# A graph and attention layer: where its rows are normalised and its edge lists made, and how its first chunks are multiplied

## The chip, the cores and the metric

The kernel runs on one core of a Trainium2 chip. The time is device microseconds (us) of one execution of the whole program. Engines are called as in the profile: PE (TensorE, matrix products), DVE (VectorE), ACT (ScalarE), POOL (GpSimd), SP (SyncE, which here only issues DMAs). The three timed runs of the kernel before took 3303.76, 3309.79 and 3318.09 us.

## What is computed

x has 10000 rows of 512 numbers (float32). There are 160000 edges, sorted by their destination.

```python
xn = layernorm(x)
# part 1: message passing
agg = segment_sum((xn @ W)[src] * edge_weight[:, None], dst)
# part 2: linear attention, 8 heads of 64
q, k, v = split(xn @ w_qkv.T)
q = softmax(q, within a head) * 64 ** -0.5
k = softmax(k, over all rows)
out = layernorm_gamma((k.T @ v per head, applied to q) @ w_out.T)
x = x + relu(agg + bias) + out
# part 3: six experts, mixed by a router that sees the mean of layernorm(x)
x = x + experts(layernorm(x))
```

The kernel sums messages of xn itself and multiplies by W afterwards, and it forms the exponentials of q and k without subtracting a maximum. For that it needs a proof that these are small: the squared norm of each column of the weights of q and k is compared with a bound (7.0), and the answer, `usable`, is the scale of every exponential. If it is not fulfilled, or if the lists of edges are not as the fast path assumes, a branch in the middle (`general_path`) computes the general case; for these inputs it is not taken.

## The kernel before

Rows are cut into 20 chunks of 512 (128 partitions x 4 rows, the quarters; the last has 272), edges into 1250 tiles of 128.

**Rows.** `normal_rows(n)` brings in the next n chunks: SP loads x (L409), DVE forms mean and variance of each quarter (L157, L158) and adds epsilon (L160), POOL raises to the power -1/2 (L162), DVE forms the negative mean (L413), and then the quarters are normalised in place, two by POOL (L416) and two by ACT in two passes each (L419, L420). ACT's queue writes the chunk to `xn_d` in the chip's main memory (L421). The first KEPT = 2 chunks stay in buffers of their own; the others share the pool `a_io` of 4 buffers, and are read again later (`rows_of`, L800).

**First sweep over chunks.** Each chunk is transposed (`turned_rows`, L192), multiplied by the weights of k and q, and the exponentials are taken (ACT, L848). The first EARLY = 3 chunks do this with plain products (`times`, L200: 16 for k and 16 for q); the rest with Strassen's scheme in Winograd's form (`seven`, L234: 28 products), which needs sums of the weights (`kq_sum`, L224 to L227) and of the rows (`xs_b`, L217 to L220) on DVE. q is normalised on DVE (`softmax_rows`, L183 to L185), transposed, and stored in `qT_d`. `pc` (L871) adds k-transposed times xn to the context G.

**Norms of the weights.** Between K and Q of chunk 0, `norms` squares a weight on ACT, sums it over its rows on PE with a column of ones as the stationary operand (L591), and takes the largest on DVE; `as_they_are` compares, and spreads the answer over the partitions with one more product (L600).

**Edges.** `place_edges` loads four lists (source, weight, destination, first destination of each tile) and turns them on DVE into `place` (where within a window an edge adds), `bases` and `jump` (which window is where), and counts of what holds. `find_rows` finds for each chunk where its sums lie; `oddities` adds up the counts into `n_odd`, which `general_path` reads. Then come the tiles: for each, POOL gathers 128 rows of `xn_d` (L556, `msg`, 24 buffers), DVE writes a selection matrix (L562, L564), PE multiplies (L574, `pm`), ACT copies and stores the sums in `part_d` (L577, L578). Windows that reach over a boundary are joined by carries (L641, POOL's queue).

**Second sweep.** Attention's output (`po`, L200), the gathered sums of edges `at` (L963, an indirect DMA on POOL), their product with W (`pg`, L200), and x1 is stored. **Third stage:** the experts, on PE alone for nearly all of its time.

**What sets the order.** PE's instructions stand in the order in which they are written (`manual_schedule`). The orders of the other engines are set by a scheduler when the kernel is built; `behind(a, b)` tells it to put a behind b on one engine, without a wait. Each engine then runs its list strictly in order. `work(us)` is called after products, and paces two things by an estimate of PE's time: until `place_edges` has run it calls `normal_rows` so that rows are spread over the first chunks (by `EARLY_TOTAL`, with 2 chunks of lead), and from then on `edges_to`, which writes tiles into PE's order (PACE = 0.9 us per tile, from an offset of -6 tiles; PRODUCT = 0.83 us per product). Tiles not placed by the end of the first sweep go on in the second.

Of the kernel before, what the change touches and what calls it, by code (L numbers as in the profile page):

```python
# [9 lines left out]
F32 = mybir.dt.float32  # L10
# [18 lines left out]
EARLY = 3  # L29
ROWS_SOON = 5  # L30
# [20 lines left out]
def gps_layer_kernel(  # L51
# [59 lines left out]

    until = const.tile([P, P], F32, name="until")
# [40 lines left out]
    def row_stats(t, r, mv, on_pool=False):  # L153

        st = small.tile([P, SUB, nc.vector.BN_STATS_DIM], F32, name="st")
        for s in range(SUB):
            nc.vector.bn_stats(st[:r, s, :], t[:r, s, :])  # L157
# [12 lines left out]
        nc.vector.scalar_tensor_tensor(near[:r], near[:r], -0.5, ve[:r], op0=ALU.mult, op1=ALU.mult)  # L170
        nc.vector.scalar_tensor_tensor(mv[:r, :, 1], near[:r], 1.5, root[:r], op0=ALU.add, op1=ALU.mult)
# [210 lines left out]
    with ExitStack() as ph:  # L382
# [7 lines left out]
        ew = edge_ctx.enter_context(tc.tile_pool(name="edge_w", bufs=3))  # L390
# [11 lines left out]
        normal = []  # L402

        def normal_rows(n):
# [33 lines left out]
        n_big = ep.tile([1, 2], F32, name="n_big")  # L438
# [3 lines left out]
        def place_edges():  # L442
# [15 lines left out]
            nc.vector.tensor_copy(place, dst_sb)  # L458
# [54 lines left out]
        def find_rows(c, other):  # L513

            at = ew.tile([P, 1], F32, name="at")
            lo, hi = span(c)
            past = ew.tile([P, WIDEST], F32, name="past_c", bufs=1)[:, : hi - lo - 1]
# [28 lines left out]
        def edges_in(i):  # L546
# [12 lines left out]
            sel = ew.tile([P, 2 * GROUP, WIN], F32, name="sel", bufs=6)  # L559
# [8 lines left out]
        def edges_summed(i, batch, m, sel):  # L568
# [7 lines left out]
            part = ew.tile([P, D], F32, name="part")  # L576
# [8 lines left out]
        def norms(i, w):  # L585

            sq = b_io.tile([P, KB, D], F32, name="sq", tag="qT")
            nc.scalar.activation(sq, w, AF.Square)
            pn = psum_e.tile([1, D], F32, name="pn", tag="pm")
            for kb in range(KB):  # L590
                nc.tensor.matmul(pn, ones, sq[:, kb, :], start=kb == 0, stop=kb == KB - 1)  # L591
            nc.vector.tensor_reduce(n_big[:, i : i + 1], pn, axis=AX.X, op=ALU.max)

        def as_they_are():


            nc.vector.tensor_scalar(n_big, n_big, NORM2, None, op0=ALU.is_le)
            nc.vector.tensor_tensor(n_big[:, 0:1], n_big[:, 0:1], n_big[:, 1:2], ALU.mult)
            pn = psum_e.tile([P, 1], F32, name="pn", tag="pm")
            nc.tensor.matmul(pn, until[0:1, :], n_big[:, 0:1], start=True, stop=True)  # L600
            nc.vector.tensor_copy(usable, pn)

        def oddities():

            n_good = ew.tile([P, 1], F32, name="n_good", bufs=1)
# [3 lines left out]
            n = ew.tile([1, 2], F32, name="n", bufs=1)  # L609
            nc.vector.tensor_scalar(n[:, 0:1], pn, -1.0, float(ALL_GOOD), op0=ALU.mult, op1=ALU.add)  # L610
            nc.vector.tensor_scalar(n[:, 1:2], n_big[:, 0:1], -1.0, 1.0, op0=ALU.mult, op1=ALU.add)
# [10 lines left out]
        def carry_loads(i):  # L622
            on = ew.tile([P, PER, D], F32, name="on", bufs=1)
            nc.scalar.dma_start(on[:CHAINED], by_window[:CHAINED, i * PER : (i + 1) * PER, :])
            own = ew.tile([P, PER, D], F32, name="own", bufs=1)
# [3 lines left out]
        def carry_chained(i):  # L629
            on, own = held.pop("loads")  # L630
            same = ew.tile([P, P], F32, name="same", bufs=1)
# [20 lines left out]
        EARLY_TOTAL = PRODUCT * KB * EARLY * 3 * KB  # L652
# [160 lines left out]

        xn = rows_of(0)
        xnT = turned_rows(0, xn)
        for c, (_, r) in enumerate(chunks):
            if c == EARLY:
                normal_rows(NCH)
                place_edges()
                next_nodes()  # L820
                oddities()
                for soon in range(ROWS_SOON):
                    find_rows(soon, None)
                norm_ctx.close()
                done[1] = -6 * PACE
# [6 lines left out]
            if c < EARLY:  # L832
                for o, w in ((ek, wk), (qt, wq)):
                    sums = []
                    for s in range(SUB):
# [32 lines left out]
            for cb in range(KB):  # L868
# [4 lines left out]
                if c:  # L873
                    added = nc.vector.tensor_tensor(G[:, cb, :], G[:, cb, :], pc, ALU.add)  # L874
                else:
                    nc.vector.tensor_copy(G[:, cb, :], pc)
                work(SUB * PRODUCT)
                if cb == KB // 2 - 1:
                    qT = b_io.tile([P, KB, SUB * P], F32, name="qT")
                    transposed(qT, qt, r, psum, "ps")  # L880
                    nc.scalar.dma_start(qT_d[c], qT[:, :, : SUB * r])
            if c >= ROWS_SOON:
                find_rows(c, added)
            if c == EARLY - 2:
                for inst in sums_for([kq_sum[:, i] for i in range(4)], wk[:, :KH], wq[:, :KH], wk[:, KH:], wq[:, KH:]):
                    behind(inst, added)
# [524 lines left out]
```

## Time and profile before

| what | us |
|---|---|
| median of three runs | 3309.79 |
| profiled execution, its own time | 3313.32 |
| its span in the trace | 3311.6 |
| PE busy in the span | 3206.1 |
| POOL busy | 1387.6, of which gathers 1230.9 |
| DVE busy, ACT busy | 1773.9, 822.0 |
| first products of chunk 0 (K) | at 18.7 |
| products of chunk 3, the first with Strassen | at 178.8 |
| first gather; first tile's products | at 173.8; 194.5 |
| last gather | at 1857.5 |

The profile is one execution, recorded by the hardware. Its first part gives the busy time of each engine. The groups have one line for a source line, engine, operation and tile: "out<-in", the count, then busy us and mean ns of one, then the engine's idle time just before such instructions and what ended it. The view of waits gives, for one engine, what its instructions waited for: us in total, how often, the longest. A timeline gives start, length, engine, line, and in brackets the idle time before it with its releaser. A view of windows gives for each stretch the busy time of each engine (with the number of instructions), the granted clock of PE, the busy share of the 16 DMA engines and GB/s; where it is limited to a tile, the busy times are those of that tile's instructions.

### The profile page before, as it was taken

What the parts mean: (1) busy time and instruction counts of PE and PEld (TensorE: products, weight loads), DVE (VectorE), ACT (ScalarE), POOL (GpSimd) and SP (SyncE); (2) the same over time, 40 slices, a digit from 0 to 9 for tenths busy, and PEclk for the clock granted to TensorE, in tenths of its full rate; (3) what the DMA queues carried; (4) which work ended last, traced back from release to release, by engine and by line L of the source; (5) the groups of instructions that cost most, each with busy time, mean ns of one, the idle gap of its engine ahead of it and who ended that gap; (6) DMA issues with size and microseconds to landing.
All of it is one profiled execution on the core that took longest, in us unless ns stands there. A gap on an engine that the chain in (4) does not pass through costs nothing.

```text
span 3311.6 us, 36107 instructions
## 1 busy us (share of the span) xinstructions
PE 3206.1 (97%) x12779; PEld 1893.4 (57%) x12779; DVE 1773.9 (54%) x3935; ACT 822.0 (25%) x1664; POOL 1387.6 (42%) x1416
## 2 busy tenths in 40 slices
PE   6999999999999789999999989999999999999998
PEld 3444444444443233333333358888888888888886
DVE  7855556555553256565655666445544455445533
ACT  4422222222221112222222132222222222222211
POOL 6667777777777777777777400000000000000000
PEclk9999999999999999999999989999999999999999
DMA  8778888888878899999999822222121212122111
GB/s 320 286 254 267 273 281 290 283 260 278 277 243 278 295 318 353 340 351 345 341 339 340 246 96 60 56 67 74 51 64 51 89 51 64 51 78 63 52 39 40
DMA packets 216011, 654.39 MB, mean 198 GB/s; under 512 B 34405, under 2 KB 74341, under 8 KB 188107
## 3 DMA queue, kind: packets, MB, share of 16 engines
q0 software_dynamic: 105552, 360.05, 33.7%
q1 hardware_dynamic: 67800, 169.56, 15.5%
q10 hardware_dynamic: 42464, 122.32, 9.5%
q8 instruction: 105, 1.72, 0.2%
q14 instruction: 90, 0.74, 0.1%
HBM read 491.21 MB, written 166.63 MB: 199 GB/s over the span
## 4 chain that ended last, share of the span: by engine, by line
PE 88%; DMA 8%; DVE 2%; issue 1%; POOL 1%; ACT 0%; POOLq 0%; DVEq 0%; SPq 0%; ACTq 0%
PE px L234 15%; PE p L234 12%; PE pz L234 11%; PE py L234 10%; PE pm L574 9%; PE po L200 8%; PE pg L200 8%; PE pc L871 7%; DMA msg<-xn_d,src_sb 4%; PE pt L192 3%; PE ph L234 2%; PE pk L200 2%; DMA xn<-in_x 1%; DMA z_d<-xt 1%; DMA at<-part_d,row_of 1%
## 5 line engine op out<-in xcount | busy, mean ns | idle before, releaser
L556 POOL DMA_INDIRECT msg<-xn_d,src_sb x1250 | 1230.9, 985 | 425.2 <-issue 196.5
L574 PE MATMUL pm<-msg,sel 128*32 128x512 f32 x2504 | 372.6, 603 | 19.4 <-DMA msg<-xn_d,src_sb 17.6
L200 PE MATMUL po<-G,qT 128*128 128x512 f32 (+1 forms) x640 | 297.2, 610 | 18.3 <-DMA qT<-qT_d 18.3
L200 PE MATMUL pg<-wq,aT 128*128 128x512 f32 (+1 forms) x640 | 294.1, 606 | 0.0
L871 PE MATMUL pc<-xn,ek 128*128 128x512 f32 (+1 forms) x640 | 286.4, 596 | 0.7 <-DVE G L874 0.6
L577 ACT COPY part<-pm 128x512 f32<-128x512 f32 x217 | 126.9, 585 | 611.5 <-PE pm L574 603.4
L574 PEld LDWEIGHTS pm<-msg,sel 128*32 128x32 f32 x2504 | 69.1, 109 | 288.1 <-issue 186.3
L200 PEld LDWEIGHTS po<-G,qT 128*128 128x128 f32 (+1 forms) x640 | 116.3, 190 | 186.2 <-issue 162.6
L200 PEld LDWEIGHTS pg<-wq,aT 128*128 128x128 f32 (+1 forms) x640 | 115.5, 188 | 177.1 <-issue 162.2
L234 PE MATMUL px<-xnT,w_sb 128*128 128x256 f32 (+1 forms) x800 | 203.7, 377 | 11.3 <-DVE u L1228 11.1
L157 DVE BATCH_NORM_STATS2 st<-ot 128x6 f32<-128x512 f32 (+1 forms) x160 | 110.2, 689 | 190.8 <-ACT ot L1001 190.2
L871 PEld LDWEIGHTS pc<-xn,ek 128*128 128x128 f32 (+1 forms) x640 | 117.0, 190 | 142.1 <-issue 130.8
L234 PE MATMUL p<-kq_sum,xs_b 128*128 128x512 f32 (+1 forms) x408 | 189.5, 600 | 0.0
L234 PE MATMUL px<-w_sb,hh 128*128 128x256 f32 (+1 forms) x800 | 185.7, 379 | 0.0
L234 PE MATMUL py<-xs,w_sum 128*128 128x256 f32 (+1 forms) x800 | 185.0, 374 | 0.0
L234 PE MATMUL py<-w_sum,hh 128*128 128x256 f32 (+1 forms) x800 | 179.2, 379 | 0.0
L234 PEld LDWEIGHTS px<-xnT,w_sb 128*128 128x128 f32 x800 | 150.4, 191 | 32.7 <-DVE u L1228 13.1
L234 PEld LDWEIGHTS px<-w_sb,hh 128*128 128x128 f32 (+1 forms) x800 | 150.0, 188 | 22.7
L234 PEld LDWEIGHTS py<-w_sum,hh 128*128 128x128 f32 (+1 forms) x800 | 150.0, 188 | 22.7
L234 PEld LDWEIGHTS py<-xs,w_sum 128*128 128x128 f32 x800 | 149.4, 190 | 19.6
L345 ACT ACTIVATE xn<-xn,st_all 128x128 f32<-128x128 f32 x288 | 114.8, 481 | 99.8 <-DMA xn<-x_d 92.1
L234 PEld LDWEIGHTS p<-kq_sum,xs_b 128*128 128x128 f32 (+1 forms) x408 | 73.6, 187 | 109.7 <-issue 84.4
(299 smaller groups left out, 4649.8 us busy)
## 6 DMA issues: line engine op xcount, KB each, us to landing
part_d<-part ACTq DMA_DIRECT2D x217, 256.0 KB
msg<-xn_d,src_sb POOLq DMA_INDIRECT x1250
xn<-in_x SPq DMA_DIRECT2D x19, 1024.0 KB
xn_d<-xn ACTq DMA_DIRECT2D x19, 1024.0 KB
qT_d<-qT ACTq DMA_DIRECT2D x19, 1024.0 KB
qT<-qT_d SPq DMA_DIRECT2D x19, 1024.0 KB
xt<-in_x SPq DMA_DIRECT2D x19, 1024.0 KB
x_d<-ot SPq DMA_DIRECT2D x19, 1024.0 KB
```

The source lines that it names most:

```text
L157: nc.vector.bn_stats(st[:r, s, :], t[:r, s, :])
L192: nc.tensor.transpose(pt[:, s * r : (s + 1) * r], t[:r, s, kb * P : (kb + 1) * P], ident[:r, :r])
L200: nc.tensor.matmul(po[:r, :], t[:, kb, s * r : (s + 1) * r], w[:, kb, :], start=kb == 0, stop=kb == KB - 1)
L234: nc.tensor.matmul(o, lhs[j], rhs[j], start=start and j == 0, stop=stop and j == n - 1, skip_group_check=True)
L345: nc.scalar.activation(xn[:, s, b * P : (b + 1) * P], xn[:, s, b * P : (b + 1) * P], AF.Identity, bias=st[:, b, s, 0:1], scale=st[:, b, s, ...
L556: nc.gpsimd.indirect_dma_start(out=m[k], out_offset=None, in_=xn_d, in_offset=bass.IndirectOffsetOnAxis(ap=src_sb[:, t0 + k : t0 + k + 1], ...
L574: nc.tensor.matmul(pm[h * WIN : (h + 1) * WIN, :], sel[:, k, :], m[k] if k < len(m) else m[0], start=j == 0, stop=j == batch - 1, skip_gro ...
L577: nc.scalar.copy(part, pm)
L871: nc.tensor.matmul(pc, ek[:r, s, cb * P : (cb + 1) * P], xn[:r, s, :], start=s == 0, stop=s == SUB - 1)
```

## The change

- EARLY is 2: chunk 2, the third, uses Strassen's scheme. `kq_sum` is formed at the end of chunk 1 behind its first addition to G.
- The rows are normalised by ACT alone, one pass for each quarter with scale and bias; POOL forms the bias (minus mean times the power), and adds epsilon. DVE keeps only the statistics.
- `a_io` has 7 buffers (4 before); `normal_rows` runs with 4 chunks of lead (2 before), paced so as to be done after two chunks. Two more chunks are asked for before the first transposes.
- The loads of the lists are issued on SP before the load of chunk 4 (`edges_listed`); the work on DVE is put behind the last statistics of rows (chunk 19).
- `next_nodes` and `oddities` move to chunk 5, `find_rows` of chunks 0 to 4 to chunks 5 to 9. The pool for edge work opens later, after the rows' pool is closed; tiles start from an offset of -16.
- The squares of the weights are taken early, in two buffers. The norms are formed by columns: the squares are the stationary operand, ones the moving one, 16 products of one column for each weight; the comparison is made per column, summed, and added up over the partitions by a product with a matrix of ones.
- Chunks 0 and 1: all copies after transposes go to ACT.

In the kernel after, the same lines have other numbers (K and Q products at L204, Strassen at L238, transposes at L196, `pm` at L573, `qt`'s exponentials at L856).

```diff
-EARLY = 3
-ROWS_SOON = 5
+EARLY = 2
+ROWS_IN = 2
+CHECKED = 5
...
-            nc.vector.bn_aggr(mv[:r, s, :], st[:r, s, :])
+            last_stats = nc.vector.bn_aggr(mv[:r, s, :], st[:r, s, :])
         ve = small.tile([P, SUB], F32, name="ve")
-        nc.vector.tensor_scalar_add(ve[:r], mv[:r, :, 1], EPS)
+        (nc.gpsimd if on_pool else nc.vector).tensor_scalar_add(ve[:r], mv[:r, :, 1], EPS)
         if on_pool:
             nc.gpsimd.tensor_tensor(mv[:r, :, 1], ve[:r], half_neg[:r], ALU.pow)
-            return
+            return last_stats
...
-        ew = edge_ctx.enter_context(tc.tile_pool(name="edge_w", bufs=3))
+        a_io = norm_ctx.enter_context(tc.tile_pool(name="a_io", bufs=7))
         tmp = norm_ctx.enter_context(tc.tile_pool(name="edge_t", bufs=1))
-        a_io = norm_ctx.enter_context(tc.tile_pool(name="a_io", bufs=4))
...
-                row_stats(xt, r, mv, on_pool=True)
-                minus = small.tile([P, SUB], F32, name="minus")
-                nc.vector.tensor_scalar(minus[:r], mv[:r, :, 0], -1.0, None, op0=ALU.mult)
+                last_stats[0] = row_stats(xt, r, mv, on_pool=True)
+                nc.gpsimd.tensor_tensor(mv[:r, :, 0], mv[:r, :, 0], mv[:r, :, 1], ALU.mult)
+                nc.gpsimd.tensor_scalar(mv[:r, :, 0], mv[:r, :, 0], -1.0, None, op0=ALU.mult)
                 for i in range(SUB):
-                    if i % 2:
-                        nc.gpsimd.tensor_scalar(xt[:r, i, :], xt[:r, i, :], mv[:r, i, 0:1], mv[:r, i, 1:2],
-                                                op0=ALU.subtract, op1=ALU.mult)
-                    else:
-                        nc.scalar.activation(xt[:r, i, :], xt[:r, i, :], AF.Identity, bias=minus[:r, i : i + 1])
-                        nc.scalar.activation(xt[:r, i, :], xt[:r, i, :], AF.Copy, scale=mv[:r, i, 1:2])
+                    nc.scalar.activation(xt[:r, i, :], xt[:r, i, :], AF.Identity,
+                                         bias=mv[:r, i, 0:1], scale=mv[:r, i, 1:2])
...
-        wk = kvp.tile([P, KB, D], F32, name="wk")
-        nc.sync.dma_start(wk, w_qkv_t[:, D : 2 * D].rearrange("(k p) d -> p k d", p=P))
-        nc.sync.dma_start(wq, w_qkv_t[:, :D].rearrange("(k p) d -> p k d", p=P))
-        kq_sum = kvp.tile([P, 4, KH, D], F32, name="kq_sum", tag="wv_wo")
...
-        def place_edges():
+        def edges_listed():
             nc.sync.dma_start(src_sb, src)
             nc.sync.dma_start(w_sb, edge_w)
             dst_sb = tmp.tile([P, NET], I32, name="dst_sb", tag="whole")
             nc.sync.dma_start(dst_sb, dst)
             row_sb = tmp.tile([P, NET], I32, name="row_sb", tag="row")
             nc.sync.dma_start(row_sb, dst[0:1, :].to_broadcast([P, NET]))
-
-            nc.vector.tensor_scalar(row_sb, row_sb, 2, None, op0=ALU.arith_shift_right)
+            return dst_sb, row_sb
+
+        def place_edges(dst_sb, row_sb):
+
+            behind(nc.vector.tensor_scalar(row_sb, row_sb, 2, None, op0=ALU.arith_shift_right), last_stats[0])
...
-            nc.vector.tensor_copy(place, dst_sb)
+            behind(nc.vector.tensor_copy(place, dst_sb), last_stats[0])
...
-        def norms(i, w):
-
-            sq = b_io.tile([P, KB, D], F32, name="sq", tag="qT")
+        def squares_of(w, tag):
+            sq = b_io.tile([P, KB, D], F32, name="sq", tag=tag)
             nc.scalar.activation(sq, w, AF.Square)
-            pn = psum_e.tile([1, D], F32, name="pn", tag="pm")
-            for kb in range(KB):
-                nc.tensor.matmul(pn, ones, sq[:, kb, :], start=kb == 0, stop=kb == KB - 1)
-            nc.vector.tensor_reduce(n_big[:, i : i + 1], pn, axis=AX.X, op=ALU.max)
+            return sq
+
+        def norms(i, sq):
+
+            pn = psum_e.tile([P, KB], F32, name="pn", tag="pm")
+            for cb in range(KB):
+                for kb in range(KB):
+                    nc.tensor.matmul(pn[:, cb : cb + 1], sq[:, kb, cb * P : (cb + 1) * P], ones,
+                                     start=kb == 0, stop=kb == KB - 1)
+            nc.vector.tensor_scalar(small_norms[:, i], pn, NORM2, None, op0=ALU.is_le)
 
         def as_they_are():
 
 
-            nc.vector.tensor_scalar(n_big, n_big, NORM2, None, op0=ALU.is_le)
-            nc.vector.tensor_tensor(n_big[:, 0:1], n_big[:, 0:1], n_big[:, 1:2], ALU.mult)
+            n_small = small.tile([P, 1], F32, name="n_small", bufs=1)
+            nc.vector.tensor_reduce(n_small, small_norms, axis=AX.XY, op=ALU.add)
             pn = psum_e.tile([P, 1], F32, name="pn", tag="pm")
-            nc.tensor.matmul(pn, until[0:1, :], n_big[:, 0:1], start=True, stop=True)
-            nc.vector.tensor_copy(usable, pn)
+            nc.tensor.matmul(pn, all_ones, n_small, start=True, stop=True)
+            nc.vector.tensor_scalar(usable, pn, 2.0 * D, None, op0=ALU.is_ge)
...
-        EARLY_TOTAL = PRODUCT * KB * EARLY * 3 * KB
+        EARLY_TOTAL = PRODUCT * KB * ROWS_IN * 3 * KB
...
-                normal_rows(int(done[1] / EARLY_TOTAL * (NCH + 1)) + 2 - len(normal))
+                normal_rows(int(done[1] / EARLY_TOTAL * (NCH + 1)) + 4 - len(normal))
...
-            transposed(xnT, xn, chunks[c][1], psum, "ps")
+            transposed(xnT, xn, chunks[c][1], psum, "ps", by_act=range(KB) if c < EARLY else (1, 3))
...
+        wk = kvp.tile([P, KB, D], F32, name="wk")
+        nc.sync.dma_start(wk, w_qkv_t[:, D : 2 * D].rearrange("(k p) d -> p k d", p=P))
+        nc.sync.dma_start(wq, w_qkv_t[:, :D].rearrange("(k p) d -> p k d", p=P))
+        squared = [squares_of(wk, "qT"), squares_of(wq, "xs_b")]
+        kq_sum = kvp.tile([P, 4, KH, D], F32, name="kq_sum", tag="wv_wo")
+        normal_rows(2)
+        lists = edges_listed()
         xn = rows_of(0)
         xnT = turned_rows(0, xn)
         for c, (_, r) in enumerate(chunks):
             if c == EARLY:
                 normal_rows(NCH)
-                place_edges()
-                next_nodes()
-                oddities()
-                for soon in range(ROWS_SOON):
-                    find_rows(soon, None)
+                place_edges(*lists)
                 norm_ctx.close()
-                done[1] = -6 * PACE
+                pools["w"] = edge_ctx.enter_context(tc.tile_pool(name="edge_w", bufs=3))
+                done[1] = -16 * PACE
...
-                            norms(0, wk)
-                            norms(1, wq)
+                            norms(0, squared[0])
+                            norms(1, squared[1])
...
+                    if cb == 0:
+                        first_added = added
                 else:
                     nc.vector.tensor_copy(G[:, cb, :], pc)
                 work(SUB * PRODUCT)
                 if cb == KB // 2 - 1:
                     qT = b_io.tile([P, KB, SUB * P], F32, name="qT")
-                    transposed(qT, qt, r, psum, "ps")
+                    transposed(qT, qt, r, psum, "ps", by_act=range(KB) if c < EARLY else (1, 3))
                     nc.scalar.dma_start(qT_d[c], qT[:, :, : SUB * r])
-            if c >= ROWS_SOON:
+            if c == CHECKED:
+                next_nodes()
+                oddities()
+            if c >= CHECKED:
                 find_rows(c, added)
-            if c == EARLY - 2:
+                if c < 2 * CHECKED:
+                    find_rows(c - CHECKED, added)
+            if c == EARLY - 1:
                 for inst in sums_for([kq_sum[:, i] for i in range(4)], wk[:, :KH], wq[:, :KH], wk[:, KH:], wq[:, KH:]):
-                    behind(inst, added)
+                    behind(inst, first_added)
```

More of the change, by code (lines that the diff above doesn't have):

```diff
@@ L110, in gps_layer_kernel @@
                    allow_small_or_imprecise_dtypes=True)
+    all_ones = const.tile([P, P], F32, name="all_ones")
+    nc.gpsimd.memset(all_ones, 1.0)
     until = const.tile([P, P], F32, name="until")
@@ L397, in gps_layer_kernel @@
         norm_ctx = ph.enter_context(ExitStack())
+        a_io = norm_ctx.enter_context(tc.tile_pool(name="a_io", bufs=7))
         tmp = norm_ctx.enter_context(tc.tile_pool(name="edge_t", bufs=1))
-        a_io = norm_ctx.enter_context(tc.tile_pool(name="a_io", bufs=4))
         normal = []
+        last_stats = [None]
         def normal_rows(n):
@@ L437, in gps_layer_kernel @@
         count = ep.tile([P, 3 + len(AT_HAND) + 2 * NCH], F32, name="count")
-        n_big = ep.tile([1, 2], F32, name="n_big")
+        small_norms = ep.tile([P, 2, KB], F32, name="small_norms")
         usable = ep.tile([P, 1], F32, name="usable")
         n_odd = ep.tile([1, 1], I32, name="n_odd")
-        def place_edges():
+        def edges_listed():
             nc.sync.dma_start(src_sb, src)
@@ L513, in find_rows @@
         def find_rows(c, other):
-            at = ew.tile([P, 1], F32, name="at")
+            at = pools["w"].tile([P, 1], F32, name="at")
             lo, hi = span(c)
-            past = ew.tile([P, WIDEST], F32, name="past_c", bufs=1)[:, : hi - lo - 1]
+            past = pools["w"].tile([P, WIDEST], F32, name="past_c", bufs=1)[:, : hi - lo - 1]
             scan = nc.vector.scalar_tensor_tensor(
@@ L558, in edges_in @@
                             in_offset=bass.IndirectOffsetOnAxis(ap=src_sb[:, t0 + k : t0 + k + 1], axis=0))
-            sel = ew.tile([P, 2 * GROUP, WIN], F32, name="sel", bufs=6)
+            sel = pools["w"].tile([P, 2 * GROUP, WIN], F32, name="sel", bufs=6)
             if n < GROUP * batch:
@@ L575, in edges_summed @@
                                      start=j == 0, stop=j == batch - 1, skip_group_check=True)
-            part = ew.tile([P, D], F32, name="part")
+            part = pools["w"].tile([P, D], F32, name="part")
             nc.scalar.copy(part, pm)
@@ L583, in gps_layer_kernel @@
         held = {"edges": []}
-        def norms(i, w):
-            sq = b_io.tile([P, KB, D], F32, name="sq", tag="qT")
+        def squares_of(w, tag):
+            sq = b_io.tile([P, KB, D], F32, name="sq", tag=tag)
             nc.scalar.activation(sq, w, AF.Square)
-            pn = psum_e.tile([1, D], F32, name="pn", tag="pm")
-            for kb in range(KB):
-                nc.tensor.matmul(pn, ones, sq[:, kb, :], start=kb == 0, stop=kb == KB - 1)
-            nc.vector.tensor_reduce(n_big[:, i : i + 1], pn, axis=AX.X, op=ALU.max)
+            return sq
[6 more added lines that the diff above has]
+            nc.vector.tensor_scalar(small_norms[:, i], pn, NORM2, None, op0=ALU.is_le)
         def as_they_are():
-            nc.vector.tensor_scalar(n_big, n_big, NORM2, None, op0=ALU.is_le)
-            nc.vector.tensor_tensor(n_big[:, 0:1], n_big[:, 0:1], n_big[:, 1:2], ALU.mult)
+            n_small = small.tile([P, 1], F32, name="n_small", bufs=1)
+            nc.vector.tensor_reduce(n_small, small_norms, axis=AX.XY, op=ALU.add)
             pn = psum_e.tile([P, 1], F32, name="pn", tag="pm")
-            nc.tensor.matmul(pn, until[0:1, :], n_big[:, 0:1], start=True, stop=True)
-            nc.vector.tensor_copy(usable, pn)
+            nc.tensor.matmul(pn, all_ones, n_small, start=True, stop=True)
+            nc.vector.tensor_scalar(usable, pn, 2.0 * D, None, op0=ALU.is_ge)
         def oddities():
-            n_good = ew.tile([P, 1], F32, name="n_good", bufs=1)
+            n_good = pools["w"].tile([P, 1], F32, name="n_good", bufs=1)
             nc.vector.tensor_reduce(n_good, count, axis=AX.X, op=ALU.add)
@@ L608, in oddities @@
             nc.tensor.matmul(pn, n_good, ones, start=True, stop=True)
-            n = ew.tile([1, 2], F32, name="n", bufs=1)
+            n = pools["w"].tile([1, 2], F32, name="n", bufs=1)
             nc.vector.tensor_scalar(n[:, 0:1], pn, -1.0, float(ALL_GOOD), op0=ALU.mult, op1=ALU.add)
-            nc.vector.tensor_scalar(n[:, 1:2], n_big[:, 0:1], -1.0, 1.0, op0=ALU.mult, op1=ALU.add)
+            nc.vector.tensor_scalar(n[:, 1:2], usable[0:1], -1.0, 1.0, op0=ALU.mult, op1=ALU.add)
             nc.vector.tensor_tensor(n_odd, n[:, 0:1], n[:, 1:2], ALU.add)
@@ L622, in carry_loads @@
         def carry_loads(i):
-            on = ew.tile([P, PER, D], F32, name="on", bufs=1)
+            on = pools["w"].tile([P, PER, D], F32, name="on", bufs=1)
             nc.scalar.dma_start(on[:CHAINED], by_window[:CHAINED, i * PER : (i + 1) * PER, :])
-            own = ew.tile([P, PER, D], F32, name="own", bufs=1)
+            own = pools["w"].tile([P, PER, D], F32, name="own", bufs=1)
             nc.scalar.dma_start(own[:CHAINED], by_window[1 : CHAINED + 1, SUB + i * PER : SUB + (i + 1) * PER, :])
@@ L630, in carry_chained @@
             on, own = held.pop("loads")
-            same = ew.tile([P, P], F32, name="same", bufs=1)
+            same = pools["w"].tile([P, P], F32, name="same", bufs=1)
             nc.vector.scalar_tensor_tensor(same[:CHAINED, :CHAINED], bases[:CHAINED, 1 : CHAINED + 1], nexts[:CHAINED],
```

## The prediction

> **What bounds the kernel now.** I read the page first, then the waits of TensorE (PE), then its timeline.
>
> ```profile
> span 3311.6 us, 36107 instructions
> ...
> PE 3206.1 (97%) x12779; PEld 1893.4 (57%) x12779; DVE 1773.9 (54%) x3935; ACT 822.0 (25%) x1664; POOL 1387.6 (42%) x1416
> ...
> L556 POOL DMA_INDIRECT msg<-xn_d,src_sb x1250 | 1230.9, 985 | 425.2 <-issue 196.5
> ```
>
> PE is idle for 105 us of 3311.6. The 97% hides a second bound: the 1250 gathers on POOL, one per tile of edges. Their busy time in six stretches of 100 us of the first sweep:
>
> ```profile
> 174.00:274.00 100.00, 15.39 (x128) 3.34 (x128) 76.24 (x79) 1.00 0.83 264
> 274.00:374.00 100.00, 19.23 (x160) 4.17 (x160) 76.23 (x79) 1.00 0.85 271
> ```
>
> 79 gathers per 100 us, a pitch of 1.27 us, in every stretch: POOL never stops, and PE takes the tiles about as fast. The waits of PE say who is ahead:
>
> ```profile
> PE pm L574 <- DMA msg<-xn_d,src_sb: 17.6, 22, 1.8
> ...
> PE pn L600 <- DVE n_big L598: 9.2, 1, 9.2
> PE pt L192 <- DMA at<-part_d,row_of: 6.0, 1, 6.0
> ```
>
> The 22 waits for gathers begin at 961 us. From there to the last tile (1870 us) the chain of gathers sets the time; before and after it, PE's own work does. So two things count: when the gathers can start to flow, and how much PE work is left behind the last tile. Timelines of POOL (gathers) and PE (early part):
>
> ```profile
> 173.84 1.26 POOL L556 DMA_INDIRECT msg<-xn_d,src_sb  x1 [8.83 <-DMA xn_d<-xn]
> ```
> ```profile
> 51.93 0.58 PE L600 MATMUL pn<-n_big,until 1*128 1x1 f32 x2 [9.15 <-DVE n_big L598]
> 52.44 2.08 PE L200 MATMUL pk<-wq,xnT 128*128 128x512 f32 x2
> ...
> 86.45 13.90 PE L200 MATMUL pk<-wk,xnT 128*128 128x512 f32 x32
> ...
> 133.78 6.60 PE L200 MATMUL pk<-wk,xnT 128*128 128x512 f32 x15
> ```
>
> Chunk 0 ends at 86.45, chunk 1 at 133.78. Chunk 2 (plain) ends at 178.6.
>
> **The change, step by step.** T0 is the time at which PE begins the products of chunk 2, which are now Strassen's: 133.8 before.
>
> *Step 1, the first rows.* All four quarters of a chunk now go through ScalarE (ACT) once: 4 x 0.62 = 2.5 us, as much as two quarters twice before. POOL loses 2 x 2.07 us per chunk and gains three small operations that the trace doesn't show in this form; a 128x4 memset takes 0.10, the 128x4 power 1.03, so between 0.3 and 3.1 per chunk. They resemble the 0.10 row (plain arithmetic): 0.3. DVE loses two of 0.07 pitch. These edits are hidden by the loads. But in the built order ACT has the rows of chunks 0 to 3 and both squares (1.9 each) ahead of the four copies that turn chunk 0. The x of chunk 3 lands at 23.3 (its first statistics); + 2.8 statistics + 1.5 POOL + 2.5 ACT = 30.1, + 0.6 copy: K of chunk 0 starts at 30.8, against 18.68. With its 15.0 us it ends at 45.8.
>
> *Step 2, norms.* 64 records with one column. The nearest row is the sum of the keys at the end of the sweep (8 records in 0.95 us): 64 x 0.119 = 7.6 us, against 2 x 3.59 = 7.2; the squares are ready long before. They end at 53.4. Then PE waits for the count on DVE, and behind that wait stand all products of Q. On DVE the count stands, in the built order, behind three quarters of the statistics of chunk 10. What must have moved by then: eleven chunks of x (11.5 MB), two weights (2.1), four lists (2.6), constants (0.7), 16.9 MB read, with 4.2 to 7.3 MB written. The rate at this place is 404 GB/s and the engines are full:
>
> ```profile
> 25.00:50.00 25.00, 15.78 (x37) 4.70 (x35) 15.61 (x46) 11.38 (x14) 19.86 (x13) 0.96 0.98 404
> ```
>
> By 0.38 to 0.40 MB per us chunk 10 lands at 53 to 63, so the factor for the exponentials exists at 56 to 66. I take 65, because the moved list loads (2.6 MB) stand before chunk 4 on SP. The wait is 11.6 us, against 9.15. Q as before 0.5 + 16.9, then the rest of chunk 0 (69.2 to 86.45 before, 17.2): chunk 0 ends at 99.8, chunk 1's K and Q (27.6) at 127.5.
>
> *Step 3, lists behind the last statistics.* The listing on DVE costs, by its rows: shift 0.78, casts and gap 4, nodes and jump 2.5, three by-window pairs 4.7, three fused 1250-wide 4.3, the four smaller 3.5, 53 small counts at 0.065 pitch 3.4: 23 us. In the built order they, kq_sum (5.2) and the copies, softmax and adds of chunk 1 stand ahead of the last normalised quarter of Q of chunk 1: 34.6 us from the end of the last statistics, and 24.9 us from the copy that waits for PE's first transposes of chunk 2. Before, the list lay beside chunk 1 and 2, hidden under PE. Chunk 19's load stands on SP behind chunk 2's reload, which waits for the end of chunk 0 (99.8); two loads and the statistics later it is 110 to 117. So 117 + 34.6 = 152, or 127.5 + 1.9 + 24.9 = 154: the later one. PE would be ready to transpose Q at 127.5 + 1.9 + 6.9 = 136.3: a new stall of about 17 us. Then 1.75 + 6.87: 162.6.
>
> *The clock.* The 9.15 us of idle before Q was followed by 10.2 us at a granted clock of 0.5, and Q took 16.94 us instead of 13.90: 3.0 lost. The new stall costs between 1 and 3; T0 = 164, bounds 154 to 172. The Trainium skill, "TensorE: Matmul & The Clock Gate", Part 1, says that one idle window of about 3.4 us halves the rate, and some 3.4 us of work restores it. This speaks against a second stall; by it one would lose 1.7 us, but the row shows a stretch three times as long, so the sum goes by the row.
>
> *Step 4, chunk 2.* 28 products instead of 32 in place of plain ones: 4 x 0.86 = 3.4 us saved on PE. The first tile stands behind all 28 (24.1 us) in PE's order.
>
> *Step 5, gathers and the end.* With all of xn_d written at 125 to 128 POOL may start, but 24 buffers are full after 30.4 us, and are freed only by tiles at T0 + 24 + 2. So the chain acts as if started at T0 + 26 - 30.4 = T0 - 4 = 160, against 173.8: 14 earlier. Yet PE's order now has 712 tiles in the first sweep instead of 680, and behind the last tile stand 96 matmuls and 64 transposes up to the end of the second sweep, where before there were 60 and 48: 36 x 0.86 + 16 x 0.11 = 32.7 us of work that no longer lies beside gathers. The wait for `at` (6.0) falls away, since POOL is done with tiles a lap sooner. Sum: -13.8 + 32.7 - 6.0 = **+13**. As a check, PE alone: (164 - 133.8) - 3.4 - 17.6 - 6.0 = +3; the chain is later, so it decides. What hides the moved searches for rows and the oddities (chunks 5 to 9, some 1 us each): DVE is half idle there (0.52 busy from 178.6 to 1117).
>
> The profiled execution took 3313.3 us, so 3326; by the median shown (3309.8) **3323**.
>
> **Rivals.** *A, as above* (T0 154 to 172; +4 to +21). *B, faster: neither gate holds.* If loads come early and DVE gets through the list beside chunk 1, T0 = 30.8 + 15.0 + 7.6 + 34.0 + 47.4 = 135, and the sum is -16; with the copies of chunk 0 not held by chunk 3 either, -28. For it: DVE was busy 42 of 47 us in chunk 1, so nothing is slow there but order. Against: the order is fixed, and 34.6 us do not fit before 136 unless the last statistics end by 102. *C, slower: the last statistics.* From 119 us on (154 - 34.6) each us by which they end later is paid 1:1. Seven places do not help if the engines are full; before, the last load was issued at 144.7 and landed 9.5 later:
>
> ```profile
> 154.23 1.28 DVE L157 BATCH_NORM_STATS2 st<-xn 68x6 f32<-68x512 f32 x2 [6.58 <-DMA xn<-in_x]
> ```
>
> Half of the way from there (135) gives T0 = 180, +29. *D, slower: gathers are not the chain*, but PE is, and its 23.6 us of waits stay, since the pace in PE's order still runs ahead of POOL: 30.2 - 3.4 = +27.
>
> **Chances.** A 0.47, B 0.20, C 0.22, D 0.11. 0.5% (16.5 us) is about what a measurement here can tell from no change. Of A 0.06 lies over it, of B 0.04 within. Faster 0.16; same 0.47 - 0.06 + 0.04 = 0.45; slower 0.22 + 0.11 + 0.06 = 0.39. The range 3290 to 3345 takes in A, B to -20 and C and D to +35, and leaves about 0.15 out.
>
> **What would show it.** K's first products at 30 to 31 us; PE waiting 10 us or more for the DVE count at about 65; a stall of 15 us or more before the transposes of chunk 1's Q, released by DVE; the first gather at 125 to 128, then POOL waiting for PE after 24; first tile at 185 to 190; last gather some 14 us earlier, and no wait for `at`. If Q's transposes don't wait, step 3 is wrong; if the last gather moves earlier by 30 or more, step 5's start is.

## The result and the profile after

The changed kernel took 3340.72 us (median of 4 runs, 3334.89 to 3342.97), the kernel before 3310.14: a ratio of 1.009, 95% interval 1.0074 to 1.0105. It is slower by 30 us, where +13 was forecast and -20 to +35 was the range. The profiled execution took 3342.77 us, its span is 3341.0. The experiments ran on several chips: on some the kernel before took 3306 to 3313 us, as here, on others 3568 to 3575; each ratio below is to the kernel before on the same chip, and the 8% between the chips is a finding of its own.

The page, the lines that answer to those of before:

```profile
span 3341.0 us, 36157 instructions
...
PE 3207.3 (96%) x12819; PEld 1906.2 (57%) x12819; DVE 1772.5 (53%) x3902; ACT 833.8 (25%) x1674; POOL 1328.8 (40%) x1437
...
L555 POOL DMA_INDIRECT msg<-xn_d,src_sb x1250 | 1238.1, 990 | 431.8 <-issue 206.2
```

PE works as long as before (3207.3 against 3206.1 us); 28.1 of the 29.4 us by which the span grew are idle time of PE. The windows say where. First the kernel before, up to the products of chunk 2, and the 800 us from 200 on (columns: stretch, length, PE busy, granted clock, share of the DMA engines, GB/s):

```profile
0.00:133.78 133.78, 106.05 (x290) 0.96 0.83 319
...
200.00:1000.00 800.00, 798.22 (x3117) 1.00 0.84 272
```

And the changed kernel:

```profile
0.00:173.25 173.25, 117.81 (x339) 0.87 0.78 302
...
200.00:1000.00 800.00, 800.00 (x3123) 1.00 0.84 274
```

| | before | after | |
|---|---|---|---|
| chunk 2's products begin | 133.8 | 173.3 | +39.5 |
| PE idle up to there | 27.7 | 55.4 | +27.7 |
| PE at work up to there | 106.1 | 117.8 | +11.8 |
| PE idle from there to the end | 77.8 | 78.2 | +0.4 |
| PE at work from there to the end | 3100.0 | 3089.5 | -10.5 |

The idle time is the start's alone. The 11.8 us of longer work for the same products are a lower clock (0.87 against 0.96) and dearer norms; of the 10.5 us regained, 3.4 are the four products that Strassen's scheme saves, the rest lies mainly in the groups of tiles (372.6 us busy then, 359.6 now). A second profile of the kernel before (`b_before`, below) has 366.2 us there, so about half of that difference is no more than two executions of one kernel differ by.

The waits of PE in the changed kernel:

```profile
PE po L204 <- DMA qT<-qT_d: 20.3, 3, 8.3
PE pm L573 <- DMA msg<-xn_d,src_sb: 16.7, 14, 3.0
...
PE pk L204 <- ACT xnT L198: 13.2, 1, 13.2
PE pt L196 <- DVE xnT L198: 11.6, 2, 6.6
PE pt L196 <- DVE qt L189: 8.2, 3, 5.5
PE pg L204 <- ACT aT L198: 5.9, 1, 5.9
PE pt L196 <- DVE G L886: 5.6, 1, 5.6
```

The waits for `xnT`, `aT` and `G` are new, that for `qt` was 1.2 us before; all but the one for `aT` lie before chunk 2. Its timeline gives the places:

```profile
31.67 16.47 PE L204 MATMUL pk<-wk,xnT 128*128 128x512 f32 x32 [13.22 <-ACT xnT L198]
47.98 11.49 PE L594 MATMUL pn<-ones,sq 128*128 128x1 f32 x64
62.27 0.56 PE L604 MATMUL pn<-n_small,all_ones 128*128 128x1 f32 x2 [2.79 <-DVE n_small L602]
...
139.38 1.97 PE L196 MATMUL pt<-ident,xn 128*128 128x128 f32 x8 [6.58 <-DVE xnT L198]
146.37 1.12 PE L196 MATMUL pt<-ident,xn 128*128 128x128 f32 x4 [5.03 <-DVE xnT L198]
...
161.04 0.45 PE L196 MATMUL pt<-ident,qt 128*128 128x128 f32 x1 [5.49 <-DVE qt L189]
...
173.25 1.88 PE L238 MATMUL p<-kq_sum,xs_b 128*128 128x512 f32 x4
```

13.2 us for the copies of chunk 0, which stand on ACT behind chunk 3's rows; 2.8 for the norms; 5.6 for the first copy of G, which stands on DVE behind statistics; 19.2 for copies and softmax that stand on DVE behind the last statistics and inside the list. DVE at that place:

```profile
116.74 2.47 DVE L161 BATCH_NORM_STATS2 st<-xn 128x6 f32<-128x512 f32 x4 [10.83 <-DMA xn<-in_x]
...
126.81 1.88 DVE L161 BATCH_NORM_STATS2 st<-xn 68x6 f32<-68x512 f32 x3 [7.32 <-DMA xn<-in_x]
128.61 0.36 DVE L162 BATCH_NORM_AGGREGATE mv<-st 128x2 f32<-128x6 f32 x4
...
130.35 0.77 DVE L449 TENSOR_SCALAR row_sb<-row_sb 128x1250 int32<-128x1250 int32 x1
...
162.72 0.69 DVE L189 TENSOR_TENSOR qt<-qt,qs 128x512 f32<-128x512 f32 x1
```

Chunk 18 is in at 116.7 and chunk 19 at 126.8, the list begins at 130.4, and the last normalised quarter of Q comes out 33 us later.

### The profile page after: what moved, and what is told of

It is laid out like the page before. It is cut to its first block, busy times and chain, and to the rows that moved or that the text cites. A ratio compares the mean times of both kernels' runs of the same rounds, so it can differ in the third digit from the quotient of the medians.

```text
span 3341.0 us, 36157 instructions
## 1 busy us (share of the span) xinstructions
PE 3207.3 (96%) x12819; PEld 1906.2 (57%) x12819; DVE 1772.5 (53%) x3902; ACT 833.8 (25%) x1674; POOL 1328.8 (40%) x1437
## 4 chain that ended last, share of the span: by engine, by line
PE 57%; DMA 7%; DVE 1%; issue 0%; ACT 0%; POOL 0%; DVEq 0%; ACTq 0%; POOLq 0%
PE px L238 14%; PE pz L238 10%; PE py L238 9%; PE po L204 8%; PE pg L204 8%; PE pm L573 4%; DMA msg<-xn_d,src_sb 2%; PE ph L238 2%; DMA z_d<-xt 2%; DMA xt<-x_d 1%; PE pt L196 1%; DMA qT<-qT_d 1%; DVE xt L1305 0%; DMA x_d<-ot 0%; DMA part_d<-part_d 0%
## 5 line engine op out<-in xcount | busy, mean ns | idle before, releaser
L573 PE MATMUL pm<-msg,sel 128*32 128x512 f32 x2504 | 359.6, 603 | 17.3 <-DMA msg<-xn_d,src_sb 16.7
L204 PE MATMUL po<-G,qT 128*128 128x512 f32 (+1 forms) x640 | 298.3, 612 | 20.3 <-DMA qT<-qT_d 20.3
L204 PE MATMUL pg<-wq,aT 128*128 128x512 f32 (+1 forms) x640 | 294.8, 608 | 5.9 <-ACT aT L198 5.9
L204 PEld LDWEIGHTS po<-G,qT 128*128 128x128 f32 (+1 forms) x640 | 116.8, 191 | 189.2 <-issue 167.0
L573 PEld LDWEIGHTS pm<-msg,sel 128*32 128x32 f32 x2504 | 66.3, 109 | 274.6 <-issue 184.5
L204 PEld LDWEIGHTS pg<-wq,aT 128*128 128x128 f32 (+1 forms) x640 | 116.2, 189 | 183.9 <-issue 164.1
L238 PE MATMUL px<-xnT,w_sb 128*128 128x256 f32 (+1 forms) x800 | 204.1, 378 | 13.8 <-DVE u L1243 13.6
L238 PE MATMUL p<-kq_sum,xs_b 128*128 128x512 f32 (+1 forms) x432 | 200.7, 600 | 0.0
L238 PE MATMUL px<-w_sb,hh 128*128 128x256 f32 (+1 forms) x800 | 185.7, 379 | 0.0
L238 PE MATMUL py<-xs,w_sum 128*128 128x256 f32 (+1 forms) x800 | 185.6, 375 | 0.0
L238 PE MATMUL py<-w_sum,hh 128*128 128x256 f32 (+1 forms) x800 | 179.2, 379 | 0.0
L238 PEld LDWEIGHTS px<-xnT,w_sb 128*128 128x128 f32 x800 | 150.1, 191 | 37.0 <-DVE u L1243 17.4
L238 PEld LDWEIGHTS py<-w_sum,hh 128*128 128x128 f32 (+1 forms) x800 | 150.0, 188 | 22.7
L238 PEld LDWEIGHTS px<-w_sb,hh 128*128 128x128 f32 (+1 forms) x800 | 150.0, 188 | 22.7
L238 PEld LDWEIGHTS py<-xs,w_sum 128*128 128x128 f32 x800 | 150.0, 191 | 20.0
L238 PEld LDWEIGHTS p<-kq_sum,xs_b 128*128 128x128 f32 (+1 forms) x432 | 78.0, 187 | 116.1 <-issue 89.9
```

The source lines that it names most:

```text
L204: nc.tensor.matmul(po[:r, :], t[:, kb, s * r : (s + 1) * r], w[:, kb, :], start=kb == 0, stop=kb == KB - 1)
L238: nc.tensor.matmul(o, lhs[j], rhs[j], start=start and j == 0, stop=stop and j == n - 1, skip_group_check=True)
L573: nc.tensor.matmul(pm[h * WIN : (h + 1) * WIN, :], sel[:, k, :], m[k] if k < len(m) else m[0], start=j == 0, stop=j == batch - 1, skip_gro ...
```

## The experiments

Two theories. **S**: PE's own path sets the time; what it loses before chunk 2 passes to the end. **T**, the prediction's step 5: the chain of gathers sets it, from the first tile to the last, plus the work that stands behind the last tile in PE's order.

**1. Less work behind the last tile** (`f_pace`), and the kernel before beside it (`b_before`).

```diff
-PACE = 0.9
+PACE = 0.94
```

> The changed kernel with PACE 0.94 instead of 0.9: the first tile stands where it stood in PE's order, each later one a little later, so that 41 us less of products are left behind the last tile. Nothing else. Theory T (last gather plus the work behind it; the gathers set their own pace from the first tile on): the last gather comes when it came, and the time falls by 30 to 41 us. Theory S (PE's path: the same work, the same idle at the start): the gathers are held back by PE, the last one comes 30 to 40 us later, and the time changes by 0 to -10 us.

> The kernel before, for its profile on the chips of these runs (3572 to 3575 us there, 3310 in the first measurement). What is to be seen: whether its first 200 us are as in the first profile (chunk 2 at 134, first tile at 194), and so whether the 39 us by which the changed kernel begins chunk 2 later are lost there too and regained elsewhere. Theory S on such a chip: the loss is regained between 200 and 2000 us, in which all engines show waits without a releaser (PE busy 90% of that time instead of 97%); theory T: last gather of the kernel before no earlier than the changed kernel's 2061, less work behind it.

Measured: 3344.16 us, 1.010 (1.008 to 1.0119), as the changed kernel; the kernel before 3306.49, its chunk 3 at 178.8, its first tile at 194.4, as in the first profile. In `f_pace`, 63.5 us stand behind the last tile instead of 102.7, but the last gather, POOL's timeline:

```profile
1874.80 0.94 POOL L555 DMA_INDIRECT msg<-xn_d,src_sb  x1 [1.59 <-DMA msg<-xn_d,src_sb]
```

came at 1874.8 instead of 1845.4, 29.4 us later. PE holds the gathers back, and what is saved behind is lost ahead. T falls on this chip. Of S, its first half stands, that PE's own path sets the time; this edit leaves the start as it is, so it does not test the second half.

`b_before` ran on a chip like the first, so what its expectation asks of the slower chips stays open. It shows how far two executions of one kernel differ. Its last gather:

```profile
1845.73 0.95 POOL L556 DMA_INDIRECT msg<-xn_d,src_sb  x1 [0.30 <-issue]
```

came 11.8 us sooner than in the first profile of the same kernel, and no later than in the changed kernel (1845.4), whose first gather came 17.6 us sooner (154.2 against 171.8). From the products of chunk 2 to the end it took 3171.1 us, the first profile 3177.8, the changed kernel 3167.8 and `f_pace` 3164.0. The four products saved are 3.4 of that; the rest is of the size by which the two profiles of the kernel before differ (6.7). So from chunk 2 on the changed kernel is not the slower one; what it loses, it has lost by then.

**2. Lists not behind the last statistics** (`e1_free`, and again as `e1b_free` beside the changed kernel).

```diff
-            behind(nc.vector.tensor_scalar(row_sb, ...), last_stats[0])
+            nc.vector.tensor_scalar(row_sb, ...)
...
-            behind(nc.vector.tensor_copy(place, dst_sb), last_stats[0])
+            nc.vector.tensor_copy(place, dst_sb)
```

> The listing of edges is no longer put behind the last statistics, so DVE does it as soon as the lists have landed, beside chunk 0. Theory S (the start: what PE loses before chunk 2 passes to the end): the 25 us of PE idle between 132 and 166 us shrink to about 5 (the last chunk's statistics at 130 and ACT's rows still stand before the exponentials of Q), chunk 2 begins at 150 to 155 instead of 173.3, and the time falls by 18 to 23 us, to about 3320. Rival L (the late landing of chunk 19, not the list, holds PE): chunk 2 begins at 165 or later and the time is above 3330. Rival T (work left behind the last tile decides, the start is slack): no change, 3335 to 3343.

> As e1_free (the listing of edges not put behind the last statistics), again, beside the changed kernel. Theory S (idle before chunk 2 passes to the end): chunk 2 begins some 10 us sooner than in the changed kernel (163.6 in the run before, against 173.3) and the time is 8 to 12 us below the changed kernel's, a ratio of 1.006 to the kernel before on a chip like the first. Rival T (the start is slack, work behind the last tile decides): equal to the changed kernel within 3 us.

Measured: 3568.45 (0.9988, 0.9967 to 1.001) and 3565.79 (0.9978, 0.9957 to 0.9999). Chunk 2 began at 163.6 and 166.6 instead of 173.3: the list's place costs 7 to 10 us of the start, not 20. The two values lie on either side of rival L's mark of 165. Of the 30 to 33 us by which chunk 2 is still later than in the kernel before, 20 to 24 are there when chunk 1 begins (at 106.6 and 110.9, against 86.5): K's late start, and PE's wait at the end of chunk 0 for DVE's copies of G (7.9 and 12.1 us). The rest comes after it. The end can't tell S from T here: `e1b_free` is 7 us below the changed kernel on the same chip (the next run), near S's 8 to 12, but the intervals of the two ratios overlap.

**3. the control** (`c_after`, the changed kernel unchanged).

> The changed kernel itself, once more, beside the others on one chip, since the chip of the first four runs took 3575 us for the kernel before, 8% more than the one of the first measurement. On a chip like the first: 1.009 times the kernel before. On a chip like the second, where every engine of the first two stages shows short waits that have no releaser in the profile and gathers come at 66 per 100 us instead of 79, the start's loss can be hidden: 0.998 to 1.006.

Measured: 3573.04, 0.9992 (0.9971 to 1.0013): on this chip the change costs nothing that can be told, though chunk 2 begins at 173.28 as before. POOL's gathers there, in stretches of 100 us (columns: length, PE, weight loads, POOL with the number of gathers, clock, DMA, GB/s):

```profile
274.00:374.00 100.00, 20.46 (x144) 4.37 (x144) 66.94 (x70) 1.00 0.78 248
474.00:574.00 100.00, 20.20 (x144) 4.27 (x144) 65.14 (x68) 1.00 0.72 222
674.00:774.00 100.00, 15.39 (x128) 3.34 (x128) 61.34 (x63) 0.91 0.71 222
```

63 to 70 gathers instead of 79, and PE waits for something without a releaser:

```profile
PE pm L573 <- issue: 30.9, 33, 4.3
PE pg L204 <- issue: 26.7, 16, 4.3
```

From first to last tile it takes 1891 us there, on the first chip 1660.

**4. Chunk 0 turned first** (`e2_turn`), and with the lists free (`e6_both`).

```diff
-        normal_rows(2)
-        lists = edges_listed()
         xn = rows_of(0)
         xnT = turned_rows(0, xn)
+        normal_rows(2)
+        lists = edges_listed()
```

> Chunk 0 is turned before the rows of chunks 2 and 3 are asked for, so the four copies no longer stand behind those rows on ACT. K of chunk 0 begins at about 19 us instead of 31.7, and the count of the norms stands behind chunk 7's statistics instead of chunk 10's: Q at 50 to 52 instead of 62.7. Theory S: 10 to 12 us earlier at chunk 2, and the time falls by as much, to about 3330. Rival L (the landing of the last chunks sets it): chunk 19 lands as before, chunk 2 begins at 170 or later, within 3 us of 3341. Rival T: no change.

> Chunk 0 turned before the rows of chunks 2 and 3, and the lists not behind the last statistics: both edits of the first call together. Q of chunk 0 begins at about 52 and the list lies beside chunk 0 and 1. Theory S: chunk 2 begins at 155 or sooner and the time is 18 to 23 us below the changed kernel's, about 1.003 times the kernel before on a chip like the first. Rival L (the last chunk's rows, which stand on ACT before the exponentials of Q, hold PE): chunk 2 at 160 or later, 10 us gained at most.

Measured: 3573.03 (1.0001, 0.9981 to 1.0022) and 3568.16 (0.9989, 0.997 to 1.0008). K began at 22.7, not 19, and Q at 51.5, 11 us sooner, as expected; but chunk 2 at 170.2 and 164.8: of the 11 us, 3 were left against the changed kernel, 2 against `e1b_free` and none against `e1_free`. In `e6_both` the gain is eaten here (PE's wait, and a window of it with the busy times of PE, weight loads, DVE, ACT and POOL):

```profile
96.47 0.90 PE L196 MATMUL pt<-ident,qt 128*128 128x128 f32 x3 [18.86 <-DVE G L886]
```
```profile
80.00:96.00 16.00, 0.00 (x0) 0.00 (x0) 16.00 (x38) 2.90 (x4) 5.58 (x8) 0.59 0.57 233
```

DVE is at work without a pause: statistics of rows, the list and the softmax stand ahead of its copies of G. So chunk 1 begins at 109.3, where the changed kernel beside it begins it at 104.5, and the last two loads, which SP issues behind the end of chunk 0, go out at 110.0. Rival L's marks (170 and 160) came true; at the end of chunk 0 it is the order on DVE that holds PE, and the late landing follows from it.

**5. Tiles 32 places later** (`e3_off48`, and again as `e3b_off48`).

```diff
-                done[1] = -16 * PACE
+                done[1] = -48 * PACE
```

> Tiles start 32 places later in PE's order (offset -48 instead of -16); nothing else. Theory T (last gather plus the work behind the last tile sets the end): 30 us of products come back beside gathers, the time falls by 25 to 33 us, to about 3312. Theory S (PE's path, with its idle at the start): PE's work is the same, only waits for gathers (16.7 us) and what stands at the end (9.6 us of waits for queries and for ACT) can go, so between 0 and -20 us, 3321 to 3341; most likely about -10, with the waits for gathers gone.

> As e3_off48 (tiles start 32 places later in PE's order), again, beside the changed kernel. Theory T (last gather plus the work behind the last tile): 25 to 33 us below the changed kernel. Theory S (PE's path): 0 to 20 us below, most likely about 10, since only the waits for gathers and the waits at the end of the second sweep can go.

Measured: 3573.87 (1.0004, 0.9981 to 1.0027) and 3576.92 (1.0001, 0.9981 to 1.0021). The edit was badly chosen: it moves the first tile too (228.4 instead of 197.4), so under T the gathers beyond the first 24, which the buffers hold, go on 31 us later, and 34 us are saved behind the last tile (66.1 instead of 100.1). No change is what T should have expected too, and the edge of S's range, so the run can't tell them apart.

**6. Chunk 2 plain again** (`e5_early3`).

```diff
-EARLY = 2
+EARLY = 3
```

> EARLY back to 3 with all else of the change: chunk 2 uses plain products (3.4 us more on PE), the lists are not needed before chunk 3. Theory S: the copies after chunk 2's and Q's transposes go to ACT, so the list on DVE holds PE only through Q's softmax of chunk 1; some 12 of the 25 us of idle go, 3.4 come: about 3332. Theory T: tiles start a chunk later in PE's order with the same offset, about 36 tiles, the work behind the last tile shrinks by 32 us: about 3310. If the lists were the whole of it, chunk 2's products begin at 150 or sooner.

Measured: 3591.68, 1.0053 (1.0024 to 1.0082). Neither theory as expected: chunk 2 at 165.5, tiles from 234.3, 37 us later than in the changed kernel, 34.5 us less behind the last tile, and 1915 us between first and last tile. It is slower than the kernel before clear of noise, and no run shows why.

**7. The change without its squeeze** (`h_spread`), and **the kernel before with the norms first on DVE** (`g_norms`).

```diff
-EARLY = 2
-ROWS_IN = 2
+EARLY = 3
+ROWS_IN = 3
...
-                normal_rows(int(done[1] / EARLY_TOTAL * (NCH + 1)) + 4 - len(normal))
+                normal_rows(int(done[1] / EARLY_TOTAL * (NCH + 1)) + 2 - len(normal))
...
-        normal_rows(2)
...
-                done[1] = -16 * PACE
+                done[1] = -6 * PACE
```

(with the edits of runs 2 and 4), and, to the kernel before:

```diff
-            nc.vector.bn_stats(st[:r, s, :], t[:r, s, :])
+            stats = nc.vector.bn_stats(st[:r, s, :], t[:r, s, :])
+            if on_pool and "usable" in first and len(first["rows"]) >= 6:
+                behind(stats, first["usable"])
```

(and the two beginnings of the list behind `usable` as well).

> The change without its squeeze: rows are again spread over three chunks with two of lead, Strassen from chunk 3, tiles from -6, lists not behind the last statistics, chunk 0 turned first; kept are ACT's normalising alone, seven places, the norms by columns with early squares, the copies on ACT and the later searches. Theory S: K at 23, Q at about 50, products of chunk 2 at 125 to 135 as in the kernel before, and the time is that of the kernel before within 8 us (0.997 to 1.002), 25 to 35 below the changed kernel. Rival K (what was kept costs the time: ACT's queue, in which rows and exponentials stand in one line): chunk 2 begins at 145 or later and the ratio is 1.005 or more.

> The kernel before with one edit of order: on DVE the lists and the statistics of chunks 6 to 19 stand behind the factor for the exponentials. Chunk 6 lands at 43.8, so nothing is held up for long. Theory S (what PE loses before chunk 2 passes to the end): the wait of 9.15 us for the count shrinks to about 1, Q begins at 44 to 45 instead of 52.4 and no longer at half clock, chunk 2 begins 8 to 11 us sooner, and the time falls by as much: a ratio of 0.997 on a chip where the kernel before takes 3310. Theory T (gathers decide): the first gather is no sooner, the last one no sooner, no change within 2 us. On a chip where the kernel before takes 3570 the two can't be told apart.

Measured: 3573.96 (1.002, 0.9999 to 1.0041) and 3559.41 (0.999, 0.997 to 1.001), on a chip with 3568 for the kernel before. In `h_spread` chunk 2 begins at 137.1, 36 us sooner than in the changed kernel and 3 later than in the kernel before, and chunk 1 at 84.5 (104.7 in the changed kernel, 86.5 before): the squeeze made most of the loss of the start, not ACT's normalising. Rival K falls by both its marks, though chunk 3 begins at 188.7, still 10 us behind the kernel before. The 25 to 35 us below the changed kernel that S expected don't show: on a chip of the same kind that kernel had 0.9992, so the 36 us are not seen at the end there. In `g_norms` the wait for the count fell from 9.15 to 1.15 us:

```profile
44.50 0.38 PE L604 MATMUL pn<-n_big,until 1*128 1x1 f32 x2 [1.15 <-DVE n_big L602]
```

Q began at 44.8 and took 14.0 us, and chunk 2 began at 125.3 instead of 133.8, the 8 us that were expected. Whether they reach the end on a chip like the first was not measured; here the interval holds both.

## Why the prediction was right and wrong

Its sign and range held, its sum did not. By its own mark of 0.5% the change is slower, to which it gave 0.39, against 0.45 for the same.

| step, as the prediction put it | predicted | measured |
|---|---|---|
| K of chunk 0 begins | 30.8 | 31.7 |
| 64 norm products | 7.6 | 11.5 |
| Q begins | 65 | 62.7 |
| chunk 0 ends | 99.8 | 104.7 |
| last statistics end | 110 to 117 | 130.4 |
| chunk 2 (T0) | 164 (154 to 172) | 173.3 |
| first gather | 125 to 128 | 154.2 |
| last gather, against before | -13.8 | -12.2 |
| from it to the last tile's products | 0 | -1.0 |
| behind the last tile, to the end of the second sweep | +32.7 - 6.0 | +36.5 (with 3.7 for queries and 5.9 for `aT`) |
| third stage | 0 | +6.0 |
| sum | +13 | +29.4 |

*Right:* the three gates, each with the engine that was named, and the order behind them; the stall at the list is 19.2 us for 17. One sign failed: PE waited 2.8 us for the count, not 10 or more, since the products of the norms ended 6 us later than forecast. The 24 buffers held POOL, which waited 9.5 us for the first tile's products. Rival C's mechanism came true: 130.4 is 11 us past its point of 119, and T0 is 9 us past 164. So did rival D's: PE is the chain and its waits stay, for which the prediction had +27. It gave the two 0.22 and 0.11; that 30 us lie inside the range is owed to the width that was made for them.

*Luck:* the last gather, -12.2 for -13.8. By the step's own rule the measured T0 would give some -5, and against `b_before` the last gather is 0.4 us earlier.

*Wrong, step 3:* "two loads and the statistics later it is 110 to 117". The loads were issued at 105.4, behind the end of chunk 0, and landed at 116.7 and 126.8. Between 100 and 117 the DMA engines had a share of 0.96, since ACT had let go of its backlog of written rows; from 117 to 127 the share was 0.70, so what held the second load is shown in part only. The prediction had this rate in a fence and used it for chunk 10, but not here.

*Wrong, step 5:* "the chain of gathers sets the time". Experiment 1 shows that it does not on such a chip: work moved from behind the last tile to ahead of it leaves the time as it was, since PE's work and its idle time at the start remain. The prediction's other sum, PE alone, is the one that holds: with T0 = 173.3 it gives 39.5 - 3.4 = 36.1, less what waits fall away (the span grew by 29.4, and by 36.2 against `b_before`). It subtracted all 23.6 us of waits; 0.4 more were idle in the end, because other waits came (2.0 more for queries, 5.9 for `aT`, 2.5 more for `u` in the third stage) where that for `at` (6.0) went, and the waits for gathers stayed (16.7 against 17.6). What fell was hidden in busy time: 13.0 us in the tiles' groups, 6.4 of which also lie between the two profiles of the kernel before.

*Mis-sized:* the norms, 11.5 for 7.6 (8.8 to 11.6 in the runs that form them by columns).

Shown, then: PE's added idle time lies before chunk 2, and the squeeze of the rows into two chunks makes most of it. `e6_both`, with the lists free and chunk 0 turned first, begins chunk 1 at 109.3; `h_spread`, which spreads the rows as well, at 84.5. `h_spread` also sets EARLY to 3, so the two are not taken apart at chunk 2; EARLY alone (`e5_early3`) left it at 165.5. Argued from the sums of four profiles, and not tested by changing the start alone on a chip like the first: that the loss passes whole to the end. Open: why other chips take 8% longer and then hide the loss.

## What to carry to other kernels

Before a list of who waits for whom, add up the bytes: rows that are to be loaded, normalised and written in two chunks' time need the DMA engines for longer than those chunks last (an estimate: 20.5 MB in and 20.5 MB out at the 404 GB/s of the prediction's window are 101 us, and two chunks of 47 us are 95), and then every engine that works in order holds unrelated work behind data still under way: DVE waited 10.8 and 7.3 us for the last two chunks. Where two chains run side by side, ask which has idle time in the middle; PE had 800 us without a gap, and the gathers followed it (experiment 1), so its start is what should count. Test such a claim by an edit that moves one term only.

## What was not expected of the hardware

*Products of one column let the clock fall.* PE was at work without a gap from 48.0 to 59.5, yet the granted clock fell in the midst of the norms, which began at 48.0 (columns: stretch, length, PE busy, clock, DMA share, GB/s):

```profile
46.00:50.00 4.00, 4.00 (x24) 1.00 1.01 428
50.00:52.00 2.00, 2.00 (x13) 0.58 1.02 426
52.00:54.00 2.00, 2.00 (x11) 0.50 1.03 430
```

It stayed at 0.50 until 66, and Q took 16.3 us after a wait of only 2.8. The norms by whole rows in `g_norms` kept 1.00 throughout. In `f_pace` the clock fell only between 52 and 54, and the same products took 8.8 us instead of 11.5. The Trainium skill, "TensorE: Matmul & The Clock Gate", Part 1, says that the gate follows how busy the array was in a window of some 3.4 us; a fall 2 to 6 us into the norms is not at odds with that, if such products count as idle, which no run isolates.

*POOL slowed beside the list.* With DVE working through the list without a pause, the power on a 128x4 tile took 7.07 us instead of 1.04, and ACT waited 13.2 us until chunk 18's bias was there (POOL, then ACT):

```profile
130.31 7.07 POOL L166 TENSOR_TENSOR mv<-ve,half_neg 128x4 f32<-128x4 f32 x1
```
```profile
138.85 2.93 ACT L419 ACTIVATE xn<-xn,mv 128x512 f32<-128x512 f32 x4 [13.21 <-POOL mv L417]
```

Some 8 of the 13.2 us are POOL's. The others are order: chunk 18 landed at 116.7, but DVE forms its mean (128.61, shown above) only behind the statistics of chunk 19. In `e1b_free`, where the list lies earlier, POOL's work for the last two chunks took 5.5 us instead of 13.2, and the first gather came at 151.1, 3 us sooner, though POOL began that work 3 us later. So of the 26 us by which the first gather missed its prediction some 8 are POOL's, and most of the rest is the later landing. The Trainium skill, "Trainium Architecture — The Big Picture", What this means for kernel authors, says that DVE and GpSimd share a pair of ports into the on-chip memory under an exclusive lock; the two times of the power agree with that, though no run isolates the ports.

*Chips differ.* The kernel before had medians of 3310 and 3313 us in two measurements and of 3568 to 3575 in three others. In the profiles of the changed kernel each DMA queue moves the same bytes on both kinds of chip, and on the slower one all engines show waits that the profile gives no releaser for.
